# Sending the block outputs of a mixture-of-experts layer to their tokens' places instead of gathering them, with the blocks, the norming, the zeros and the first scores moved

## The chip, the cores and the metric

The kernel runs on one core of one Trainium2 chip. The core has a matrix engine (TensorE, PE in the profile, with PEld for its weight loads), three further engines (VectorE or DVE, ScalarE or ACT, GpSimd or POOL), a queue engine (SyncE or SP) that here only issues transfers, and 16 DMA engines that all queues share. PE, DVE, ACT, POOL and SP each run their own instructions strictly in order and wait for one another on semaphores. The metric is the time of one execution in microseconds (us), as the median of several runs.

## The reference

The input `x` has 8 batches of 512 tokens of 128 features. Four layers follow one another, each of the form

```python
xn = layernorm(x)                 # per token, no gain or bias
x = x + attention_L(xn) + ffn_L(xn)
```

Layer 0: causal attention with 16 heads of 8 features, and a mixture of 16 experts of which each token uses 4:

```python
logits = -sum((x[:, :, None] - keys) ** 2, -1) + x @ rw.T + rb
topv, topi = top_k(logits, 4);  w = softmax(topv)
hidden = gelu(x @ w1[e].T + b1[e]);  out[e] = hidden @ w2[e].T + b2[e]   # 128 -> 512 -> 128
fused = sum over the 4 chosen e of w[e] * out[e]
```

Layer 1: linear attention (8 heads of 64, a decayed running sum over the tokens, a gate), and a mixture of 8 experts of which each token uses one, weighted by its probability:

```python
a, g = split(x @ w1[e], 2);  y = (silu(a) * g) @ w2[e]                  # 128 -> 2*512 -> 128
```

Layer 2: causal attention and an adapter that each batch chooses out of 8; layer 3: attention with a position bias and two of 8 small networks per batch. Layers 2 and 3 are not touched by the change. All arithmetic is in float32.

## The kernel before

**Attention of layer 0.** A *unit* is one batch and one group of four heads: 8 x 4 = 32 units, numbered 4b + g. `stream` (L747) works through them in six steps each. In its steps a unit gets transposed scores (L628), their exponentials on ACT (L669), the products with the values (L687), and at the unit's end a copy (L698) and a division (L721, L724). The row maxima that the exponentials need come from a first set of scores (L556, with the causal mask by L574) and DVE's maxima (L588); this first set runs AHEAD = 5 units in front. The loads of heads for both sets (`sq`, `sk`, `tq`, `tk`) are issued on SP by `load` (L541). In units whose `select` is true, the diagonal is masked on POOL by an affine select (L673) rather than on PE.

**Dispatch to the experts** is the class `Dispatch` (L199 and on), used once for layer 0 (`d0`) and once for layer 1 (`d1`):

- `route` (L260) finds the chosen experts of a batch on DVE, `count` (L308) numbers the tokens of each expert, and `plan` (L329) gives each expert a whole number of *blocks* of 256 tokens (79 blocks for layer 0, 23 for layer 1).
- `fill` (L230) writes zeros over the last block of every expert and over the unused tail in the DRAM table `tok`, by DMAs on SP whose addresses are read into registers (L225, L253).
- `place` (L369) computes each token's slot, and `scatter` (L393) sends the normed rows to their slots: one POOL indirect DMA for 128 rows (L396), 128 of them for layer 0 and 32 for layer 1.
- `owners` (L349) computes which expert each block belongs to. It compares running block counts with the block numbers `kk`, which POOL writes by an iota (L355). `weights` (L287) computes the mixing weights.
- `tokens` (L403) loads a block from `tok` on SP (L406), and waits for the scatters. `expert` (L411) loads the block's weights (L415).
- A block is turned (`turn_tokens`, L434), multiplied (L965 and L967 hold the hidden layer of layer 0, L1284 that of layer 1), and `out_product` (L443) makes the output on PE (L448), adds the bias on DVE (L452, layer 0) or copies on ACT (L454, layer 1) into one of two `ys` buffers, and stores the rows as they stand to the DRAM table `y` by SP (L455).
- `gather` (L418) brings back the rows of 128 tokens by POOL indirect DMAs, one for each choice (L422, 160 in all), and `combine` (L427) adds them to `x` with their weights on DVE (L430, 128 rows of 128 features each, 4 per batch and tile in layer 0).

**Order of the work.** For PE, DVE and ACT the order of instructions is written out by hand (`tc.manual_schedule`, L1547); SP's and POOL's order is chosen by the scheduler of the framework, from the program and its buffers. Tiles with the same tag share a fixed number of buffers, so that a tile waits until an earlier one with its tag has been read. `start0` (L870) norms, routes, plans, fills, places and scatters for layer 0 at the very start; normed rows come from DVE for batches 0 and 1 and from POOL for the others (`apply`, L175). Then `stream` runs the 32 units. `at0(u, h, f)` attaches other work to step h of unit u: the next batch's projections (for batch b at unit 4(b-2)), `owners` at unit 1, `weights` at unit 2. The blocks of layer 0 run inside the units 13 to 22 (`START, SPAN = 13, 10`, so `END0` is 23), 79 blocks in ten units.

From unit 23 on, *spots* are counted: one per step, first over the rest of layer 0's units (`FIRST1 = (32 - END0) * 6`, 54 spots), then six for each of the 32 units of layer 1 (`unit1`, L1310), and two more units. `at_spot(s, f)` attaches work to a spot: the gathers of layer 0 at spots 3n, their combines at 3n + 1 two gathers later (32 each, to spot 100), layer 1's routing of batch b at spot 12b + 17, its plan at 108, its blocks from 140, every three spots, its gathers and combines after the last block. The normed rows of layer 1 are put into DRAM (`xd`, L1068) and read back twice: by `reload` (L1082) as `xc` for the scatters and as `xr` by `again1` (L1108) for the attention of the next batch. Both use the tag `xs`. A layer-1 unit ends with `add1` (L1252, L1260).

Of the kernel before, what the change touches and what calls it, by code (L numbers as in the profile page):

```python
# [10 lines left out]
F32 = mybir.dt.float32  # L11
# [8 lines left out]
P = 128  # L20
# [10 lines left out]
BT = 256  # L31

# [6 lines left out]
def network(ctx: ExitStack, tc: tile.TileContext, io: dict):  # L39
# [59 lines left out]
    steps256 = const.tile([P, 16], F32, name="steps256")  # L99
    nmx = [const.tile([P, NI, P], F32, tag=f"nmx{k}", name=f"nmx{k}") for k in range(2)]  # L100
# [16 lines left out]
    def tables_routing():  # L117
# [11 lines left out]
            before, before, pattern=[[-1, 16], [1, 16]], compare_op=ALU.is_ge, fill=1.0, base=0, channel_multiplier=0  # L129
        )  # L130
# [43 lines left out]

    def apply(b, engine, xn):  # L175
        mv, rt = normal[b]
        for i in range(NI):
            engine.tensor_scalar(
                xn[:, i, :], x[b][:, i, :], mv[:, i, 0:1], rt[:, i : i + 1], ALU.subtract, ALU.mult
            )  # L180
        return xn
# [5 lines left out]
    def turn_norm(L, b, xn, tag="xnT", bufs=3):  # L187
        pt = one_of(f"xt{L}_{b}")
        for i in range(NI):
            nc.tensor.transpose(pt[:, blk(i)], xn[:, i, :], ident)  # L190
        xnT[b] = wk.tile([D, T], F32, tag=tag, name=f"xnT{L}_{b}", bufs=bufs)
        nc.scalar.copy(xnT[b], pt)
# [3 lines left out]
    NOSYNC = mybir.DependencyInfo(mybir.DependencyClass.NoSync, mybir.DependencyReason.DATA)  # L196

    class Dispatch:


        def __init__(self, L, E, K, nblk, room):
# [14 lines left out]
            self.tok = dram.tile([nblk * BT + 4096 + E * BT, D], F32, name=f"tok{L}", tag=f"tok{L}", bufs=1)  # L216
            self.y = dram.tile([nblk * BT, D], F32, name=f"y{L}", tag=f"y{L}", bufs=1)
            self.scattered, self.fetched, self.got = [], [], {}
# [11 lines left out]
        def fill(self, zero):  # L230


            E = self.E
            wide = zero.shape[1] // D * P
            tails = -(-(self.nblk - NB * NI * P * self.K // BT) * BT // wide)
            last = small.tile([1, 16], F32, tag="f_last", name=f"fl{self.L}", bufs=1)[:, :E]
            nc.vector.tensor_scalar(last, self.end, float(BT), -float(BT), ALU.mult, ALU.add)
            sp = small.tile([1, 16], F32, tag="f_sp", name=f"fsp{self.L}", bufs=1)[:, :E]
            nc.vector.tensor_scalar(sp, steps256[0:1, :E], float(self.nblk * BT + 4096), None, ALU.add)
            nc.vector.tensor_tensor(sp, sp, last, ALU.subtract)  # L240
            at = small.tile([1, E + 8], F32, tag="f_at", name=f"fat{self.L}", bufs=1)
            nc.vector.scalar_tensor_tensor(at[:, :E], self.nb[0:1], 0.0, sp, ALU.is_equal, ALU.mult)
            nc.vector.tensor_tensor(at[:, :E], at[:, :E], last, ALU.add)
            for r in range(tails):
                nc.vector.tensor_scalar(
                    at[:, E + r : E + r + 1], self.end[:, E - 1 : E], float(BT), float(wide * r), ALU.mult, ALU.add
                )
            ai = small.tile([1, E + 8], mybir.dt.int32, tag="f_ai", name=f"fai{self.L}", bufs=1)
            nc.vector.tensor_copy(ai[:, : E + tails], at[:, : E + tails])
            for e in range(E + tails):  # L250
                n = BT if e < E else wide
                r = self.register(ai[0:1, e : e + 1], self.nblk * BT + 4096 + E * BT - n)
                d = nc.sync.dma_start(  # L253
                    self.tok[bass.ds(r, n)].rearrange("(p a) d -> p (a d)", p=P), zero[:, : n // P * D]
                ).ins
                self.fetched.append(d.name)
                tc.declare_no_dep(d, group=f"fill{self.L}", reason="zeros over zeros")
                tc.add_to_no_dep_group(f"fill{self.L}", d)

        def route(self, b, lg):  # L260
# [10 lines left out]
            idx = small.tile([P, NI, K], F32, tag="r_idx", name=f"ridx{n}")  # L271
# [57 lines left out]
        def plan(self):  # L329
            L, E = self.L, self.E  # L330
            n = self.run[:, NB]
            gt = small.tile([P, E, 16], F32, tag="r_tab", name=f"gt{L}", bufs=1)
# [8 lines left out]
            bf = small.tile([P, E, E], F32, tag="r_tab", name=f"bf{L}", bufs=1)  # L341
# [3 lines left out]
            self.end = small.tile([1, E], F32, tag="r_end", name=f"end{L}", bufs=1)  # L345
            nc.vector.tensor_tensor(self.end, self.base[0:1], nb[0:1], ALU.add)
            nc.vector.tensor_scalar(self.base, self.base, float(BT), None, ALU.mult)

        def owners(self):  # L349

            L, E = self.L, self.E
            le = wk.tile([P, 2 * T], F32, tag="p", name=f"le{L}", bufs=6)[0:1].bitcast(BF16)[:, : self.nblk * E]
            le = le.rearrange("p (k e) -> p k e", e=E)
            kk = small.tile([1, self.nblk], F32, tag="r_kk", name=f"kk{L}", bufs=1)
# [5 lines left out]
                self.end.unsqueeze(1).to_broadcast([1, self.nblk, E]),  # L360
                kk.unsqueeze(2).to_broadcast([1, self.nblk, E]),
                ALU.is_le,
            )
            ef = small.tile([1, self.nblk], F32, tag="r_ef", name=f"ef{L}", bufs=1)
            nc.vector.tensor_reduce(ef, le, AX.X, ALU.add)
            self.eb = small.tile([1, self.nblk], mybir.dt.int32, tag=f"r_eb{L}", name=f"eb{L}", bufs=1)
            nc.vector.tensor_scalar(self.eb, ef, float(E - 1), None, ALU.min)

        def place(self, b0, n):  # L369
# [3 lines left out]
            at = small.tile([P, 4 * NI * 16], F32, tag="r_at", name=f"at{name}", bufs=1)[:, : n * NI * E]  # L373
# [1315 lines left out]
```

## Time and profile before

| What | Value |
|---|---|
| runs | 2900.8, 2902.2, 2893.13 us; median 2900.8 |
| profiled execution | 2873.46 us |
| its span, first to last instruction | 2871.7 us, mean granted TensorE clock 0.876 |
| PE busy | 2446.5 us, 85% of the span |
| DVE / ACT / POOL busy | 1429.6 / 1191.7 / 616.1 us |
| POOL: scatters of layer 0 to their slots; gathers | L396 x128, 123.6 us; L422 x160, 153.5 us |
| DMA | 292.71 MB, mean 102 GB/s |

The profile comes from one execution, which was 27 us shorter than the median of the runs. Busy time is the time in which an engine works on an instruction; a row such as "x128 | 123.6, 965" gives the number of instructions, their busy time in us and the mean of one in ns. In a list of waits, "A L1 <- B L2: 10.0, 3, 5.0" means that instructions of line L1 on engine A waited for line L2 on engine B for 10.0 us in total, 3 times, at most 5.0 us. SPq is SP's queue of DMA issues. Lines are those of the kernel before, unless said otherwise.

### The profile page before, as it was taken

What the parts mean: (1) busy time and instruction counts of PE and PEld (TensorE: products, weight loads), DVE (VectorE), ACT (ScalarE), POOL (GpSimd) and SP (SyncE); (2) the same over time, 40 slices, a digit from 0 to 9 for tenths busy, and PEclk for the clock granted to TensorE, in tenths of its full rate; (3) what the DMA queues carried; (4) which work ended last, traced back from release to release, by engine and by line L of the source; (5) the groups of instructions that cost most, each with busy time, mean ns of one, the idle gap of its engine ahead of it and who ended that gap; (6) DMA issues with size and microseconds to landing.
All of it is one profiled execution on the core that took longest, in us unless ns stands there. A gap on an engine that the chain in (4) does not pass through costs nothing.

```text
span 2871.7 us, 45766 instructions
## 1 busy us (share of the span) xinstructions
PE 2446.5 (85%) x17798; PEld 1601.0 (56%) x17798; DVE 1429.6 (50%) x2976; ACT 1191.7 (41%) x1740; POOL 616.1 (21%) x897
## 2 busy tenths in 40 slices
PE   5660889989998868589998888888889999999999
PEld 3330447878775546477776544444445555555554
DVE  5630443333335456345555866655556655555550
ACT  1020335546555422223332145545444545555556
POOL 7475000000004553400003432222222000000000
PEclk6565789999998888799998979999888989999999
DMA  4342225666663211413322332322222222123211
GB/s 130 126 140 84 89 89 177 204 185 192 189 183 107 80 47 41 131 44 97 92 74 67 107 95 95 101 91 91 91 91 82 94 83 83 59 83 98 83 49 35
DMA packets 219000, 292.71 MB, mean 102 GB/s; under 512 B 27170, under 2 KB 112674, under 8 KB 218658
## 3 DMA queue, kind: packets, MB, share of 16 engines
q1 hardware_dynamic: 208546, 268.81, 30.2%
q0 software_dynamic: 10240, 20.99, 2.4%
q8 instruction: 141, 2.31, 0.3%
q14 instruction: 73, 0.60, 0.1%
HBM read 204.90 MB, written 84.80 MB: 101 GB/s over the span
## 4 chain that ended last, share of the span: by engine, by line
PE 69%; ACT 10%; POOL 7%; issue 6%; DVE 5%; DMA 2%; SPq 1%; ACTq 0%; DVEq 0%; POOLq 0%
PE o L687 11%; PE y L448 7%; ACT p L669 6%; PE t L628 5%; PE s L556 5%; PE h L965 5%; POOL tok L396 5%; PE t L640 5%; PE t L659 4%; PE h L1284 3%; PE s L574 2%; PE s L583 2%; PE qk L1126 2%; PE o L1213 2%; PE ot L707 2%
## 5 line engine op out<-in xcount | busy, mean ns | idle before, releaser
L588 DVE TENSOR_REDUCE max<-s 128x2 f32<-128x1024 f32 (+3 forms) x768 | 716.3, 953 | 676.8 <-PE s L574 447.9
L669 ACT ACTIVATE p<-t 128x1024 f32<-128x1024 f32 (+1 forms) x384 | 338.1, 881 | 572.3 <-PE t L640 286.0
L556 PE MATMUL s<-sk,sq 32*128 32x512 f32 (+3 forms) x1536 | 336.6, 463 | 115.0 <-DMA sk<-apartk 89.5
L628 PE MATMUL t<-tq,tk 32*128 32x512 f32 (+3 forms) x1536 | 339.9, 472 | 81.0 <-ACT p L669 74.0
L669 ACT ACTIVATE p<-t,rsc 128x1024 f32<-128x1024 f32 x256 | 281.1, 1116 | 216.6 <-PE t L659 162.1
L687 PE MATMUL o<-p,vpad 128*32 128x512 f32 (+3 forms) x3072 | 335.5, 580 | 0.2 <-ACT p L669 0.2
L556 PEld LDWEIGHTS s<-sk,sq 32*128 32x128 f32 x1536 | 146.4, 201 | 290.5 <-issue 183.8
L673 POOL TENSOR_SCALAR_AFFINE_SELECT p<-p 128x256 f32<-128x256 f32 x336 | 132.5, 407 | 740.1 <-ACT p L669 739.9
L640 PE MATMUL t<-mT,pick 32*128 32x512 f32 (+3 forms) x1536 | 262.0, 368 | 0.0
L422 POOL DMA_INDIRECT g<-y,slot x160 | 153.5, 959 | 471.0 <-issue 342.6
L628 PEld LDWEIGHTS t<-tq,tk 32*128 32x128 f32 x1536 | 143.9, 198 | 171.6 <-ACT p L669 132.7
L687 PEld LDWEIGHTS o<-p,vpad 128*32 128x32 f32 x3072 | 97.5, 127 | 157.2 <-issue 137.6
L448 PE MATMUL y<-ring_w,ring_h 128*128 128x128 f32 x1264 | 156.8, 281 | 15.4 <-DVE lowk L501 8.3
L448 PEld LDWEIGHTS y<-ring_w,ring_h 128*128 128x128 f32 x1264 | 148.6, 195 | 23.6 <-DVE lowk L501 8.7
L640 PEld LDWEIGHTS t<-mT,pick 32*128 32x128 f32 x1536 | 157.2, 205 | 2.4 <-issue 1.9
L965 PE MATMUL h<-t,ring_w 128*128 128x256 f32 x632 | 148.2, 383 | 2.6 <-issue 2.6
L396 POOL DMA_INDIRECT tok<-xn,slot x128 | 123.6, 965 | 70.3 <-issue 38.4
L574 PE MATMUL s<-mask_qk,ident_bf 128*128 128x128 bf16 (+1 forms) x768 | 137.1, 266 | 0.0
L659 PEld LDWEIGHTS t<-anti,hk 128*128 128x128 f32 x768 | 100.2, 199 | 50.6 <-issue 50.6
L965 PEld LDWEIGHTS h<-t,ring_w 128*128 128x128 f32 x632 | 116.5, 192 | 17.3 <-issue 3.4
L967 ACT ACTIVATE ring_h<-h,ring_w 128x256 f32<-128x256 f32 x316 | 119.4, 499 | 4.2 <-ACT ring_h L967 2.1
L659 PE MATMUL t<-anti,hk 128*128 128x128 f32 x768 | 118.9, 293 | 0.0
(276 smaller groups left out, 3470.5 us busy)
## 6 DMA issues: line engine op xcount, KB each, us to landing
ring_w<-in_f_w SPq DMA_DIRECT2D x79, 322.0 KB, 3.6
sq<-apartq SPq DMA_DIRECT2D x96, 256.0 KB, 2.6
tq<-apartq SPq DMA_DIRECT2D x96, 256.0 KB, 2.9
sk<-apartk SPq DMA_DIRECT2D x96, 256.0 KB, 4.1
tk<-apartk SPq DMA_DIRECT2D x96, 256.0 KB, 4.0
ring_w<-in_f_w SPq DMA_DIRECT2D x79, 256.0 KB, 3.6
xb<-tok SPq DMA_DIRECT2D x102, 128.0 KB, 4.4
y<-y SPq DMA_DIRECT2D x102, 128.0 KB, 2.1
```

Source lines behind the costliest of these rows:

```text
L396: d = nc.gpsimd.indirect_dma_start(self.tok, bass.IndirectOffsetOnAxis(self.slot[:, b, i, k : k + 1], 0), xs[:, i, :], None).ins
L422: nc.gpsimd.indirect_dma_start(g[:, k, :], None, self.y, bass.IndirectOffsetOnAxis(self.slot[:, b, i, k : k + 1], 0))
L448: nc.tensor.matmul(py[:, blk(t)], lhsT=h(f, t), rhs=w2[:, blk(f)], start=(f == 0), stop=(f == 3))
L556: nc.tensor.matmul(s[:, j, off : off + width], lhsT=q[r : r + 32, blk(i)], rhs=k[r : r + 32, :width], start=(n == 0), stop=not more, skip_ ...
L574: nc.tensor.matmul(s[:, j, c0:c1], lhsT=ident_bf, rhs=mask_qk[:, : c1 - c0], start=False, stop=True, skip_group_check=True,)
L588: nc.vector.tensor_reduce(m[:, i, g, 2 * pr : 2 * pr + 2], s[:, :, off : off + width], AX.X, ALU.max, negate=True)
L628: nc.tensor.matmul(s[:, h, off : off + T - q0], lhsT=k[r : r + 32, blk(j)], rhs=q[r : r + 32, q0:T], start=(n == 0), stop=False, skip_grou ...
L640: nc.tensor.matmul(s[:, h, off : off + T - q0], lhsT=pick[r : r + 32, g, :], rhs=mT[r : r + 32, q0:T], start=False, stop=not more, skip_gr ...
L659: nc.tensor.matmul(s[:, k, blk(i)], lhsT=self.bias[1 + part][:, h, blk(kind - i - 2)], rhs=self.bias[0], start=False, stop=(i == kind - 2 ...
L669: nc.scalar.activation(p, s[:, :, :width], AF.Exp, scale=self.scale)
L687: nc.tensor.matmul(st[b, g][blk(h, 32), q0:T], lhsT=vpad[b % 2][:, j, g * HG + h, :], rhs=st[b, g, kind, h // 2][:, h % 2, off : off + T - ...
L965: nc.tensor.matmul(s[:, f], lhsT=w1[:, blk(f)], rhs=xt, start=True, stop=True, skip_group_check=True)
```

## The change

- **Places travel with the rows.** A row of `tok` has 136 floats in place of 128. Layer 0's normed rows carry the four places that their four results will have, and the four expert numbers; layer 1's carry their token's place. When a block has been turned, `places` (three small DVE instructions in layer 0, one in layer 1) picks the place that belongs to the block's expert.
- **Sends and fetches in place of stores and gathers.** `out_product` no longer stores; `send` writes the 256 rows of a block to their tokens' places in `y` by two POOL indirect DMAs. `fetch` then reads the rows of 128 tokens (layer 0) or of a batch (layer 1) by one plain load on SP, where `gather` stood.
- **The timing table.** Blocks of layer 0 run in units 17 to 26, so 30 spots are left in layer 0; fetches stand at spots 2 + n, combines at 4 + n; layer 1's routing at 4b + 8, its plan at 42, its blocks from 74, every four spots. The units of layer 2's first scores begin at the last 30 spots. `owners` moves from unit 1 to unit 2, `weights` from 2 to 3.
- **Normed rows by ACT** in layers 0 and 1: `apply_act`.
- **First scores between the routing steps.** `start0` takes steps of `stream` (`next(stream0)`) between routing steps, three more of them around plan, fill and place; loads of tokens and fetches get an order-only dependence on the last head load issued (`latest`).
- **Zeros by index**: `fill` computes row numbers on DVE and writes the zeros by eight POOL indirect DMAs (four in layer 1) of 128 rows of 4352 bytes.
- `plan`, `place` and `owners` use the shared tag `p` for their temporaries; `owners` works on 128 partitions.

```diff
+ROW = D + 8
+    def apply_act(b, xn):
+        mv, rt = normal[b]
+        nm = small.tile([P, NI], F32, tag="nm", name=f"nm_{b}")
+        nc.vector.tensor_scalar(nm, mv[:, :, 0], -1.0, None, ALU.mult)
+        for i in range(NI):
+            nc.scalar.activation(xn[:, i, 0:D], x[b][:, i, :], AF.Identity, bias=nm[:, i : i + 1])
+        for i in range(NI):
+            nc.scalar.activation(xn[:, i, 0:D], xn[:, i, 0:D], AF.Copy, scale=rt[:, i : i + 1])
...
     def fill(self, zero):
-                d = nc.sync.dma_start(
-                    self.tok[bass.ds(r, n)].rearrange("(p a) d -> p (a d)", p=P), zero[:, : n // P * D]
+            for j in range(n + self.tails):
+                d = nc.gpsimd.indirect_dma_start(
+                    self.tok.rearrange("(r a) d -> r (a d)", a=8),
+                    bass.IndirectOffsetOnAxis(fx[:, j : j + 1], 0), zero, None,
                 ).ins
...
     def owners(self):
-            le = wk.tile([P, 2 * T], F32, tag="p", name=f"le{L}", bufs=6)[0:1].bitcast(BF16)[:, : self.nblk * E]
+            le = wk.tile([P, 2 * T], F32, tag="p", name=f"le{L}", bufs=6).bitcast(BF16)[:, : self.nblk * E]
-            kk = small.tile([1, self.nblk], F32, tag="r_kk", name=f"kk{L}", bufs=1)
+            kk = wk.tile([P, 2 * T], F32, tag="p", name=f"kk{L}", bufs=6)[:, : self.nblk]
             nc.gpsimd.iota(
                 kk, pattern=[[1, self.nblk]], base=0, channel_multiplier=0, allow_small_or_imprecise_dtypes=True
             )
...
     def tokens(self, k):
-            xb = wk.tile([P, 2 * D + 1], F32, tag="xb", name=f"xb{self.L}_{k}", bufs=4)[:, : 2 * D]
+            xb = wk.tile([P, 2 * ROW], F32, tag="xb", name=f"xb{self.L}_{k}", bufs=4)
+            if latest and not self.fetched:
+                tc.add_manual_dep(d, latest[-1], NOSYNC, reason="behind the loads of heads")
+        def places(self, k, xb):
+            n = BT // P
+            at = xb[:, :, D]
+            if self.K > 1:
+                m = small.tile([P, n, self.K], F32, tag="h_m", name=f"hm{self.L}_{k}")
+                nc.vector.scalar_tensor_tensor(
+                    m, xb[:, :, D + 4 : D + 4 + self.K], self.ef[:, k : k + 1], xb[:, :, D : D + self.K],
+                    ALU.is_equal, ALU.mult,
+                )
+                at = small.tile([P, n], F32, tag="h_r", name=f"hr{self.L}_{k}")
+                nc.vector.tensor_reduce(at, m, AX.X, ALU.add)
+            home = small.tile([P, n], mybir.dt.uint32, tag="h_u", name=f"hu{self.L}_{k}", bufs=8)
+            nc.vector.scalar_tensor_tensor(home, loose, float(k * BT), at, ALU.add, ALU.max)
+            self.home[k] = home
+        def send(self, k, ys):
+            home = self.home.pop(k)
+            for t in range(BT // P):
+                d = nc.gpsimd.indirect_dma_start(
+                    self.y, bass.IndirectOffsetOnAxis(home[:, t : t + 1], 0), ys[:, t, :], None
+                ).ins
+        def fetch(self, b, i=None):
+            d = nc.sync.dma_start(g, src).ins
+            for s in self.back[-16:]:
+                tc.add_manual_dep(d, s.name, SYNC, reason="rows are sent first")
-        def gather(self, b, i):
-            for k in range(self.K):
-                nc.gpsimd.indirect_dma_start(
-                    g[:, k, :], None, self.y, bass.IndirectOffsetOnAxis(self.slot[:, b, i, k : k + 1], 0)
-                )
...
-        nc.sync.dma_start(dst.rearrange("(t p) d -> p t d", p=P), ys)
+        return ys
...
-    START, SPAN = 13, 10
+    START, SPAN = 17, 10
...
     def start0():
         for b in range(NB):
+            if b >= 1:
+                for _ in range(2):
+                    next(stream0)
-            chosen[b] = d0.route(b, logits(0, b, kw, lb0, 16))
+            chosen[b] = d0.route(b, logits(0, b, kw, lb0, 16), xn0[:, b, :, D + 4 : D + 8])
-            if b:
+            if b >= 1:
+                for _ in range(2):
+                    next(stream0)
                 d0.count(b - 1, chosen[b - 1])
         d0.count(NB - 1, chosen[NB - 1])
+        next(stream0)
         d0.plan()
         d0.fill(zero)
+        next(stream0)
         d0.place(0, 4)
...
-    at0(1, 2, d0.owners)
-    at0(2, 2, d0.weights)
+    at0(2, 2, d0.owners)
+    at0(3, 2, d0.weights)
...
-    for n in range(len(fetch) + 2):
-        if n < len(fetch):
-            at_spot(3 * n, d0.gather, *fetch[n])
-        if n >= 2:
-            at_spot(3 * n + 1, d0.combine, *fetch[n - 2])
+    for n, (b, i) in enumerate(fetch):
+        at_spot(2 + n, d0.fetch, b, i)
+        at_spot(4 + n, d0.combine, b, i)
     for b in range(NB):
-        s = 12 * b + 17
+        s = 4 * b + 8
-    s = 12 * (NB - 1) + 24
+    s = 4 * (NB - 1) + 14
...
+    EACH = 4
     for k in range(d1.nblk + 1):
-        at_spot(s + 3 * k, hidden1, k, 0)
+        at_spot(s + EACH * k, hidden1, k, 0)
```

## The prediction

> **What bounds the kernel now.** I read the page's slices first, then windows of 40 us, then the waits of the stretches in which PE is idle, then single lines' start times.
>
> ```profile
> PE   5660889989998868589998888888889999999999
> POOL 7475000000004553400003432222222000000000
> PEclk6565789999998888799998979999888989999999
> ```
>
> One slice is 71.8 us. PE is the bound almost everywhere; it is not in slices 1 to 4 (0 to 287 us) and in the dips of slices 13 to 17. From slice 24 (layers 2 and 3, from about 1661 us) PE stands at 9, and the change does not reach there.
>
> ```profile
> 160.00:200.00 40.00, 35.33 (x252) 19.14 (x248) 22.22 (x42) 15.05 (x20) 30.40 (x31) 0.70 0.39 137
> 200.00:240.00 40.00, 0.83 (x8) 0.52 (x8) 0.85 (x2) 0.77 (x2) 30.52 (x32) 0.54 0.16 52
> 240.00:280.00 40.00, 0.15 (x4) 0.18 (x4) 0.00 (x0) 0.00 (x0) 21.33 (x24) 0.50 0.32 107
> 280.00:320.00 40.00, 34.67 (x258) 19.41 (x260) 17.46 (x25) 14.78 (x19) 0.00 (x0) 0.80 0.38 117
> ```
>
> The columns are the window, its length, and busy us of PE, PEld, DVE, ACT, POOL, then granted clock, DMA share, GB/s. From 202 to 280 us three engines stand still and POOL alone works. Why, the waits of 130 to 300 us and SP's own say:
>
> ```profile
> DVE max L588 <- PE s L574: 118.2, 23, 79.9
> ...
> PE s L556 <- DMA sk<-apartk: 78.8, 1, 78.8
> ```
>
> ```profile
> SPq L406 <- DMA tok<-xn,slot: 96.1, 3, 93.7
> ```
>
> SP's first token load (L406) waits 93.7 us for the last of POOL's 128 scatters, and the head loads (`sk`) of unit 8 are queued behind it. The scatters' own rows, first in 60 to 200 us, then in 200 to 280 us:
>
> ```profile
> L396 POOL DMA_INDIRECT tok<-xn,slot x74 | 71.9, 971 | 53.9 <-DMA tok<-room 31.6 <-issue 21.9 <-DMA tok<-xn,slot 0.3
> ```
>
> ```profile
> L396 POOL DMA_INDIRECT tok<-xn,slot x54 | 51.7, 957 | 16.5 <-issue 16.5
> ```
>
> One takes 0.96 us and 0.30 us of issue: 128 start 1.264 us apart, from 105.6 to 267.9 us. They wait 31.6 us for the zeros (`tok<-room`, 78 to 102 us).
>
> The other weak stretch is the end of layer 0 and the start of layer 1 (windows of 840 to 880, of 1000 to 1080 and of 1160 to 1240 us):
>
> ```profile
> 840.00:880.00 40.00, 38.25 (x326) 29.52 (x325) 14.30 (x32) 22.18 (x41) 4.90 (x11) 1.00 0.46 140
> ...
> 1000.00:1040.00 40.00, 23.61 (x172) 14.95 (x172) 19.56 (x72) 13.81 (x21) 16.52 (x18) 0.82 0.12 35
> 1040.00:1080.00 40.00, 28.08 (x214) 20.46 (x212) 24.72 (x78) 10.37 (x16) 23.43 (x25) 0.84 0.20 56
> ...
> 1160.00:1200.00 40.00, 23.92 (x176) 18.63 (x175) 14.67 (x32) 7.95 (x12) 23.52 (x25) 0.78 0.50 163
> 1200.00:1240.00 40.00, 27.18 (x167) 19.73 (x167) 9.74 (x17) 8.54 (x13) 7.51 (x8) 0.66 0.19 55
> ```
>
> The first is a block stage, PE-bound at clock 1.00. The last two hold layer 1's scatter stall (waits of 1130 to 1245 us): the reload `xr` of `again1(3)` finds no free buffer while `xc` tiles wait to be scattered.
>
> ```profile
> PE xt L190 <- DMA xr<-xd: 21.0, 1, 21.0
> ```
>
> **The change part by part.** The sum is made against the profiled execution, 2873.5 us (span 2871.7). The three runs have a median of 2900.8, 27.3 us more; I add that at the end. A difference under about 0.3% (9 us) can't be told from none.
>
> **Routing and scores interleaved.** Before, routing runs at one batch in 5.2 us (POOL's normed rows set it; DVE's own part is about 4.6), the plan stands at 75 us, and the first 30 score steps follow from 84.4 to 124.4 us, 1.33 us each. After, ACT norms (DVE keeps one small `nm` a batch, ACT eight instructions, at most eight times the 0.69 us of an L499 activation; ACT is busy 2.9 of 40 us there, so hidden), and 29 score steps stand ahead of `fill`'s index in DVE's order. Their lower price is DVE's: 16 maxima took 12.05 us, a unit's six steps 6.2, so 30 us; the upper is 29 x 1.33 = 39. Plan: 75 + 30 to 39, less 0 to 5 for the lost POOL bound, = 100 to 114 us; I take 105. The same scores vanish from behind the plan, so no work is lost; what is lost is that the scatters start later.
>
> **Zeros by index.** Eight POOL DMAs with 4.46 MB in place of SP's 20 with about the same. Before they took 24 us. At the page's best slice, 204 GB/s, 21.9 us; at the 163 GB/s of the window 80 to 120, 27.4. Equal within 3 us. POOL waits for them, SP's register loads go. Scatters start at 105 + 3 + 25 = 133 us (bounds 122 to 150).
>
> **Scatters and the new wait.** 128 x 1.264 = 162 us: done issuing at 295 (284 to 312). Now the step that decides. `owners` builds its block numbers `kk` by an iota on POOL (L401 after). Before, `kk` had a small buffer and its iota ran at 26 us. After, it lives in a shared `p` buffer, and in the order of POOL's instructions it stands behind all 128 scatters; `le` (L404 after) on DVE waits for it at the third step of unit 2. DVE runs in order: maxima, normings and the lows of `project` are queued behind `le`; PE waits for the maxima, ACT for PE. So SP's wait goes (the token loads now stand behind the head loads of unit 21), and DVE's takes its place, until 295 + 1 for the iota + 3 for `le` and its sum = 299 us. Before, everything resumed at 280 us with unit 3 in hand (L698 at 291); after, at 299 with unit 2 half done, 1.3 units behind, and a plain unit takes 17.5 us (311, 328, 346, 362). Cost: 19 + 1.3 x 17.5 = **+42 us** (30 to 60 by the bounds above). The stall itself grows from 78 to some 145 us (the interleaving brings unit 2 to 153 us instead of about 184), which is where the gain of the start goes.
>
> **Blocks four units later, sends.** A block unit takes 40 to 43 us, PE-bound, units 16 and 20 53 to 54 (the next batch is projected there and waits for `apartq`). Of the new ten only unit 20 projects a batch; the wait of unit 16 falls among plain units, where it shows no such cost: **-12** (-12 to 0). Per block one SP store goes (landing 2.1 us) and POOL gets two sends of 1.26 us in a unit's slack; `places` adds three tiny DVE instructions, about 0.5 us x 79, beside PE-bound work: 0; if that cover were gone, 40. `ys` has two buffers; a send may stand behind an affine select that waits for ACT (L673, 0.41 us), and the bias add of the block after next waits for the send's landing (2.25 us from POOL's start): **+10** (0 to 40).
>
> The row of 136 floats: its price per scatter or send is not in the trace; 0.96 us is for 128 rows of 512 B, both for scatters and for gathers. Lower end 0; upper end if POOL's time went with the bytes: 6%, +10 us on 128 scatters. I take 0, as issue seems to go by the row. The Trainium skill ("DMA: Bandwidth & Descriptors", section "How a descriptor splits into AXI transactions") says that a run starting off a 256 B boundary costs extra transactions; by it a 544 B row that starts off one moves up to 24 beats instead of 16, an estimate from that page. It would lengthen a token load by half, which is issued four blocks ahead, and leave the sum as it is. The same page (section "SWDGE vs HWDGE vs iDMA") says that DVE can lock POOL out while it writes descriptors. Here the scatters took 971 ns beside a busy DVE and 957 beside an idle one; by the rule sends beside DVE's work would cost more, by the rows nothing.
>
> **Fetches in place of gathers.** 160 POOL gathers (0.96 us each) go; 40 plain loads on SP come. The combines (4 x 0.351 us each) stay, but 32 of them now come at one spot each, 28 in units 27 to 31, with six routings of about 4 us among them: DVE gets about 28 x 1.4 + 6 x 4 = 63 us beside its own work in units that took 64 us before. **+15** (0 to 30). In exchange layer 1's first units carry none of it: they took 13 to 17 us (1068, 1085, 1098, 1118, 1132 at L1260), bare ones 13.5 to 15: **-14** (-20 to 0).
>
> **Layer 1.** Its plan is 66 spots earlier, but `again1(1)` wants its `xr` buffer 11 spots behind it, where before it had 17; the scatters of 32 x 1.26 = 40 us hold it as before: 26 us of stall becomes about 38: **+12** (0 to 20). 23 blocks at 1.5 a unit cost what 2 a unit did, about 4.5 us a block. The gather tail (1540 to 1660 us, PE 31.5 to 33.3 of 40) goes: **-10** (-20 to 0).
>
> Sum: 42 - 12 + 10 + 15 - 14 + 12 - 10 = +43; 2873.5 + 43 = 2916.5 in a profiled run; + 27.3 = **2944** against the median.
>
> **Rivals.** *Faster: the weak stretch closes.* The nine windows from 880 to 1240 us hold 88.7 us of idle PE, and PE at 37 of 40 would leave 27: 62 us to be won; the tail another 15. If the earlier routing and plain fetches win all of it, 42 - 12 - 62 - 15 = -47: 2854. For it: POOL's gathers wait on buffers there (19.5 us in 1000 to 1040). Against it: the same DVE work is packed tighter, and the layer-1 scatters remain. It decides once the terms behind the start add up to less than -42.
>
> *The DVE wait binds, and rows cost more.* If the wider rows or POOL's double work in the blocks bind at the upper ends (+10 scatters, +40 `ys`, `places` uncovered +40), 43 + 10 + 30 + 40 = +123: 3024. Against it: POOL is busy 2 to 4 tenths in the block slices.
>
> *No change.* The start's +42 is met by a half of the weak stretch: 2901.
>
> *The change does what it is said to at the start, and DVE is not held*: the SP wait of 78 us goes, the start's gain of 31 us stays: about -109 + 1 = 2793. Only if the iota ran ahead of the scatters, which the instruction order excludes; I give it 2 in 100.
>
> **How the numbers follow.** Forecast 0.58, slower rival 0.10, faster rival 0.24, unheld start 0.02, no change 0.06. The range leaves out half of the slower rival, the unheld start and a part of the faster rival's low end: 2846 to 3000. The forecast's own range is 2915 to 2980. Faster 0.26, same 0.06, slower 0.68.
>
> **What would show it.** In the profile after: `le` on DVE waiting for POOL's `kk` about 140 us; no wait of SP's token load; POOL's scatters from 133 to 295 us at 1.26 us; PE near 0 in 160 to 295; unit 3 finished near 334; PE over 39 of 40 in blocks, from about 560 us; no L422-like gathers. I am wrong if the scatters end well before 280 or cost another price, or if the stretch behind the blocks gets 60 us shorter.

## The result and the profile after

The changed kernel takes 3006.9 us (median; 2999.97 to 3013.12) against 2899.7 us: 1.039 times the time before, 95% interval 1.035 to 1.044. It is slower, as forecast, but by 107 us where the forecast had 43, and it lies 7 us above the range. The profiled execution has a span of 3006.3 us, granted clock 0.853.

The slices of the page after, 75.2 us each:

```profile
PE   6702888889898864788888888888889999999999
POOL 4475000343433204011110132222222100000000
PEclk6655778999999756899999979899888989889999
```

The third slice (150 to 225 us) has PE at 0. The windows over the start (columns as in the prediction: window, length, busy us of PE, PEld, DVE, ACT, POOL, granted clock, DMA share, GB/s):

```profile
120.00:160.00 40.00, 26.55 (x202) 13.90 (x199) 11.17 (x15) 11.51 (x14) 30.24 (x33) 0.70 0.42 133
160.00:200.00 40.00, 0.00 (x0) 0.00 (x0) 0.00 (x0) 0.00 (x0) 30.51 (x32) 0.50 0.16 56
200.00:240.00 40.00, 0.00 (x0) 0.00 (x0) 0.00 (x0) 0.00 (x0) 30.28 (x32) 0.50 0.16 56
240.00:280.00 40.00, 0.00 (x0) 0.00 (x0) 2.71 (x2) 0.00 (x0) 28.37 (x31) 0.50 0.15 52
280.00:320.00 40.00, 35.56 (x254) 20.25 (x254) 20.47 (x42) 14.66 (x20) 0.00 (x0) 0.71 0.44 142
```

and what DVE waited for there (waits of 100 to 400 us):

```profile
DVE le L404 <- POOL kk L401: 128.4, 1, 128.4
PEld t L714 <- DVE max L674: 127.5, 1, 127.5
```

There is one wait of 128.4 us, of `le` for `kk`, and PE waits behind DVE. The scatters' and the fills' own rows (minimum, median and maximum in ns, first and last start):

```profile
L442 POOL DMA_INDIRECT tok<-xn,slot x128: 954/958/967, 115.7 to 276.0; - x128
```

```profile
L299 POOL DMA_INDIRECT tok<-room,ffx x8: 947/954/1378, 100.3 to 110.0; - x8
```

A second place is the block stage (windows of 640 to 720 us, then one of the kernel before, where PE stood at 38 to 39.5 of 40 away from a change of batch):

```profile
640.00:680.00 40.00, 34.88 (x248) 29.89 (x247) 15.48 (x46) 18.06 (x37) 19.90 (x25) 0.91 0.58 183
680.00:720.00 40.00, 37.18 (x283) 29.98 (x282) 14.70 (x38) 21.77 (x44) 14.34 (x19) 1.00 0.50 155
```

```profile
680.00:720.00 40.00, 38.71 (x303) 32.28 (x302) 13.93 (x35) 22.76 (x44) 3.16 (x8) 1.00 0.65 196
```

The third is the end of layer 0 (units 28 to 31, after, then before):

```profile
1040.00:1080.00 40.00, 25.90 (x166) 16.26 (x166) 23.00 (x111) 20.07 (x46) 4.62 (x11) 0.54 0.31 93
1080.00:1120.00 40.00, 23.24 (x150) 14.01 (x146) 24.56 (x121) 15.38 (x35) 3.24 (x4) 0.54 0.26 79
```

```profile
960.00:1000.00 40.00, 37.14 (x306) 21.97 (x304) 16.82 (x78) 17.51 (x23) 27.32 (x29) 0.74 0.32 95
```

Neither PE nor DVE is full after the change, and the granted clock is 0.54, where the same units had 0.74 and 0.82 before (959 to 1023 us; the window of 1000 to 1040 us stands in the prediction). The engines wait for each other in turn, and the granted clock is lower besides.

The account is made from the start of the copy of `oT` (L698 before, L784 after), with which every unit ends. Each row is the time that the stage took in the two profiled executions:

| Stage | before, us | after, us | difference |
|---|---|---|---|
| to unit 11 | 431 | 452 | +21 |
| units 12 to 27 (all blocks in both) | 528 | 561 | +33 |
| units 28 to 31 | 64 | 115 | +51 |
| layer 1, to the first unit of layer 2 | 664 | 679 | +15 |
| the rest | 1185 | 1199 | +14 |
| span | 2872 | 3006 | +135 |

Layers 2 and 3 hold no edit apart from the start of layer 2's first scores, so I put the last +14 down to the executions: the profiled one of before was 27 us shorter than its median. A second profile of each kernel (experiment 5) supports it. Its five differences are +20, +36, +51, +26 and +4 us: the first three stages repeat within 3 us, while layer 1 and the rest trade 10 us, because layer 1 of the kernel before took 664 us in one profile and 653 in the other. What is to be explained is some 120 to 130 us in the first four stages.

### The profile page after: what moved, and what is told of

It reads as the page before. It is cut to its first block, busy times and chain, and to the rows that moved or that the text cites. A ratio compares the mean times of both kernels' runs of the same rounds, so it can differ in the third digit from the quotient of the medians.

```text
span 3006.3 us, 45917 instructions
## 1 busy us (share of the span) xinstructions
PE 2504.7 (83%) x17798; PEld 1628.0 (54%) x17798; DVE 1451.4 (48%) x3211; ACT 1230.2 (41%) x1884; POOL 653.5 (22%) x947
## 4 chain that ended last, share of the span: by engine, by line
PE 46%; ACT 8%; DVE 3%; issue 3%; DMA 1%; POOL 0%; SPq 0%; DVEq 0%; ACTq 0%; POOLq 0%
PE o L773 8%; ACT p L755 4%; PE s L642 4%; PE t L745 4%; PE t L714 3%; PE t L726 3%; PE h L1390 2%; PE qk L1230 2%; PE s L669 2%; PE o L1317 2%; PE s L1252 1%; PE y L533 1%; PE rc L1507 1%; PE v L1219 1%; PE s L660 1%
## 5 line engine op out<-in xcount | busy, mean ns | idle before, releaser
L755 ACT ACTIVATE p<-t,rsc 128x1024 f32<-128x1024 f32 x256 | 280.8, 1115 | 227.7 <-PE t L745 172.8
L773 PE MATMUL o<-p,vpad 128*32 128x512 f32 (+3 forms) x3072 | 348.4, 599 | 0.2 <-ACT p L755 0.2
L480 POOL DMA_INDIRECT y<-y,hu x204 | 196.0, 961 | 512.9 <-ACT y L539 351.5
L533 PE MATMUL y<-ring_w,ring_h 128*128 128x128 f32 x1264 | 155.0, 280 | 10.8 <-DVE y L537 6.2
L1065 PE MATMUL h<-t,ring_w 128*128 128x256 f32 x632 | 162.1, 409 | 0.0
L533 PEld LDWEIGHTS y<-ring_w,ring_h 128*128 128x128 f32 x1264 | 146.9, 194 | 18.3 <-DVE y L537 8.5
L1065 PEld LDWEIGHTS h<-t,ring_w 128*128 128x128 f32 x632 | 126.1, 208 | 18.1
```

Source lines behind the costliest of these rows:

```text
L480: d = nc.gpsimd.indirect_dma_start(self.y, bass.IndirectOffsetOnAxis(home[:, t : t + 1], 0), ys[:, t, :], None).ins
L533: nc.tensor.matmul(py[:, blk(t)], lhsT=h(f, t), rhs=w2[:, blk(f)], start=(f == 0), stop=(f == 3))
L755: nc.scalar.activation(p, s[:, :, :width], AF.Exp, scale=self.scale)
L773: nc.tensor.matmul(st[b, g][blk(h, 32), q0:T], lhsT=vpad[b % 2][:, j, g * HG + h, :], rhs=st[b, g, kind, h // 2][:, h % 2, off : off + T - ...
L1065: nc.tensor.matmul(s[:, f], lhsT=w1[:, blk(f)], rhs=xt, start=True, stop=True, skip_group_check=True)
```

## Experiments

Unless said otherwise, a kernel is the changed one with the edits named, and ratios are to the kernel before on the same chip. Experiments 1 to 3 ran on one chip (the first chip below), 4, 5 and 6 on a second, a third and a fourth; on the second, the kernel before itself took 3014 us.

**1. `kk` in a buffer of its own.**

```diff
-            kk = wk.tile([P, 2 * T], F32, tag="p", name=f"kk{L}", bufs=6)[:, : self.nblk]
+            kk = small.tile([P, self.nblk], F32, tag="r_kk", name=f"kk{L}", bufs=1)
```

> The changed kernel with one edit: kk, the list of block numbers in owners, has a small buffer of its own again, so that POOL can write it ahead of the 128 scatters. Theory (the wait of DVE's le on POOL's iota is a stall of its own, 128.4 us in the trace of the changed kernel, and nothing else stands behind it): the wait is gone, unit 3 finishes near 180 us instead of 313, and the time falls by 110 to 130 us from 3007 to about 2885. Rival (the scatters hold something else as well, such as the token loads or POOL's adds, so that the stall only moves a few units on): unit 10 finishes within 60 us of the 436 of the changed kernel, and the time falls by less than 60 us.

Measured 2892.1 us, ratio 1.001 (0.9985 to 1.003): 115 us less. Unit 3 finishes at 185 us, unit 10 at 312. Its windows, while POOL goes on scattering:

```profile
160.00:200.00 40.00, 33.94 (x266) 18.56 (x268) 18.96 (x37) 16.14 (x22) 30.47 (x32) 0.84 0.67 220
200.00:240.00 40.00, 36.74 (x264) 18.99 (x256) 17.35 (x31) 12.18 (x16) 30.32 (x32) 0.66 0.40 131
```

POOL's column is that of the changed kernel, and PE works at 34 to 37 of 40, as in the windows behind the stall. So the tag of one buffer was the whole stall, and nothing else that holds the units up waited for the scatters. This one line takes the change back to no difference.

**2. More buffers for block outputs, and stores in place of sends.**

```diff
-        ys = wk.tile([P, n, D], F32, tag="ys", name=name, bufs=2)
+        if int(name.split("_")[1]) % 2:
+            ys = wk.tile([P, NI * NH * (HD + 1)], F32, tag="gat", name=name, bufs=3)
+            ys = ys[:, : n * D].rearrange("p (t d) -> p t d", t=n)
+        else:
+            ys = wk.tile([P, n, D], F32, tag="ys", name=name, bufs=2)
```

> The changed kernel with more buffers for block outputs: odd blocks take one of the three gat buffers instead of one of the two ys buffers, so that a block output waits for the send of four or more blocks before. In the changed kernel a block unit takes 46 to 48 us against 40 to 41 in the kernel before, and DVE waits for the sends' landing. Theory (two buffers with POOL's sends, which stand behind affine selects, are what costs 6 us a block unit): block units fall to 40 to 42 us, the total by 40 to 60 us. Rival (the sends' transfers, or the lost granted clock, or the places on DVE cost it): block units stay at 46 to 48 us, total within 10 us of 3007.

```diff
         def send(self, k, ys):
-            home = self.home.pop(k)
-            for t in range(BT // P):
-                d = nc.gpsimd.indirect_dma_start(
...
+            nc.sync.dma_start(self.y[k * BT : (k + 1) * BT].rearrange("(t p) d -> p t d", p=P), ys)
...
-            d0.places(k, xb)
-            d1.places(k, xb)
```

> The changed kernel with block outputs stored as they stand by SP, as in the kernel before, and without places; the fetches read rows of y that are not the token's, so the results of both expert layers are left wrong, and POOL's sends and the three DVE instructions a block are left out. Theory (sends are what lengthens block units): block units 40 to 42 us, total 40 to 60 us below 3007; layer-1 units with blocks get 1 us shorter too. Rival (the block units are longer for another reason, such as rows of 544 B, ACT's norming or the transfers of that stage): block units stay at 46 to 48 us.

Measured 2972.3 us (1.028, 1.022 to 1.033) with more buffers and 2976.6 (1.031, 1.026 to 1.035) with stores: 35 and 30 us less than the changed kernel, under the 40 to 60 forecast for both. Units 17 to 25 take 40 to 43 us in both (54 and 53 in unit 20), against 46 to 48 (53). So sends cost nothing in themselves once they have buffers, nor do `places`. Layer 1 takes 678 us with sends and with stores, so the 1 us a unit that was forecast for it was not there. What DVE's bias add waited for from 520 to 1000 us (us, times), first in the changed kernel, then with more buffers:

```profile
  PE y L533: 95.7, 54
  DMA y<-y,hu: 42.5, 16
  DMA tq<-apartq: 24.6, 6
```

```profile
  PE y L533: 117.9, 73
  DMA y<-y,hu: 5.4, 4
```

Waiting for landed sends falls from 42.5 to 5.4 us, and the 24.6 us put down to `tq` loads go too. The add reads no `tq`, so that row was probably another wait under the name of what came last.

**3. Layer 1's routing and layer 0's combines at half the density.**

```diff
-        at_spot(2 + n, d0.fetch, b, i)
-        at_spot(4 + n, d0.combine, b, i)
+        at_spot(2 * n, d0.fetch, b, i)
+        at_spot(2 * n + 4, d0.combine, b, i)
...
-        s = 4 * b + 8
+        s = 8 * b + 12
...
-    EACH = 4
+    EACH = 3
...
-        at_spot(s + EACH * k + 3, turn1t, k + 1)
+        at_spot(s + EACH * k + 2, turn1t, k + 1)
```

> The changed kernel with layer 0's fetches and combines every two spots instead of every spot, layer 1's routing every eight spots instead of four (first at 12), its plan at spot 74 instead of 42, its blocks every three spots instead of four. Theory (units 28 to 31 take 115 us instead of 64 because routing and combines are packed so tightly that each step of their chain from engine to engine has only one spot): units 28 to 31 take 70 to 90 us, the total falls by 25 to 50 us. Rival (the tables of layer 1 and its setup, which moved with END0 into the last four units of layer 0, make these units long): they stay at 105 to 115 us, the total within 15 us of 3007.

Measured 2994.7 us, 1.036 (1.031 to 1.041): 12 us less than the changed kernel, under the forecast. Units 28 to 31 take 76 us, as the theory had it, but layer 1 takes 697 instead of 679: with three spots a block, its units with two blocks take 25 to 30 us, where before they took 22 to 25. The setup and tables of layer 1 are in the same units here as in the change, so they are not the cause of the long units 28 to 31. Routing and combines were thinned out together; what each of them costs alone is not shown here.

**4. Four kernels on the second chip.** The whole table of the kernel before (`START, SPAN = 13, 10`, and the spots of the lines that the diff removes, with `fetch` for `gather` and its combine at 3n + 7):

> The changed kernel with the whole timing table of the kernel before: blocks of layer 0 from unit 13 (START 13, 54 spots left in layer 0), fetches where the gathers stood (3n) and combines at 3n + 7, layer 1's routing at 12b + 17, its plan at 108, its blocks from 140 every three spots in the old order, layer 2 begun 7 spots behind them; sends, plain fetches, ACT norming, zeros by index, interleaved scores and the wait for kk stay. Theory (the tighter table costs 50 us in units 28 to 31 and 10 to 20 in layer 1, and saves 12 at a change of batch in the blocks): the total falls by 40 to 65 us to 2940 to 2967, units 28 to 31 take 64 to 70 us. Rival (the fetches and the ACT norming lengthen that stretch, not the table): units 28 to 31 stay over 100 us and the total within 20 us of 3007.

Layer 1's normed rows by DVE:

```diff
-        hold[b] = apply_act(b, wk.tile([P, NI, D], F32, tag="aT", name=f"xn1_{b}", bufs=3))
+        hold[b] = apply(b, nc.vector, wk.tile([P, NI, D], F32, tag="aT", name=f"xn1_{b}", bufs=3))
```

> The changed kernel with layer 1's normed rows for routing made by DVE as before (four instructions of 0.35 us a batch) in place of nm and eight ACT instructions. Theory (in units 28 to 31 the routing chain waits for ACT, which does eight instructions a batch there beside its exponentials): units 28 to 31 take 95 to 105 us instead of 115 and the total falls by 10 to 20 us. Rival (DVE, on which combines and routing meet, is what holds these units): they stay or grow by up to 6 us, the total within 10 us of 3007.

The pieces of a layer-1 block in the old order:

```diff
-        at_spot(s + EACH * k + 1, hidden1, k, 1)
-        at_spot(s + EACH * k + 2, out1, k - 1)
-        at_spot(s + EACH * k + 3, turn1t, k + 1)
+        at_spot(s + EACH * k + 1, out1, k - 1)
+        at_spot(s + EACH * k + 1, turn1t, k + 1)
+        at_spot(s + EACH * k + 2, hidden1, k, 1)
```

> The changed kernel with the pieces of a layer-1 block in the old order inside its four spots: first half of the hidden layer, then the output of the block before and the next turn, then the second half (the change has both halves side by side, then output, then turn). Theory (side by side, the second half waits on ACT and DVE, which is why 1.5 blocks a unit take 22 us, as long as two blocks did before): units with blocks take 20 to 21 us, the total falls by 15 to 30 us. Rival (they are long for another reason, such as the sends or the granted clock, which is 0.91 to 0.99 there): units stay at 22 us, the total within 8 us of 3007.

All of table, `kk` and buffers:

> The changed kernel with kk in a small buffer of its own, odd block outputs in gat buffers, and the whole timing table of the kernel before. If the three causes add up (115 us for kk and 35 for the buffers as measured one by one, 50 for the table as forecast), 3007 - 200 = about 2807 us, 3% faster than before. If they overlap, for example because an early end of the start only moves blocks into a stretch in which something else is late, the total stays over 2840.

Measured 3009, 3043, 3049 and 3010 us beside 3014 for the kernel before (ratios 0.998, 1.011, 1.012, 1.000, each about 0.005 either way). The times in the four expectations could not be tested: all four kernels, that with a free `kk` too, finish unit 0 at 245 to 255 us instead of 133. PE's instructions there, in the last kernel, and in the kernel of experiment 1 on the first chip (start, busy time, instruction, in brackets the idle time before it):

```profile
156.97 0.37 PE L740 MATMUL t<-mask_kq,ident_bf 128*128 128x256 bf16 x1 [2.43 <-issue]
159.77 0.47 PE L646 MATMUL s<-sk,sq 32*128 32x384 f32 x1 [2.43 <-issue]
```

```profile
148.41 0.60 PE L714 MATMUL t<-tq,tk 32*128 32x128 f32 x4
148.73 0.23 PE L642 MATMUL s<-sk,sq 32*128 32x128 f32 x2
```

On that chip, while POOL scatters (116 to 277 us), PE first gets a matmul every 2 to 2.8 us, from about 134 to 168 us in the last kernel, and then none until 247 us. DVE and ACT stand still as well (waits of the last kernel from 95 to 320 us; "issue" and "remote" mean that the profile shows no instruction and no transfer that ended the wait):

```profile
ACT p L759 <- remote: 164.1, 3, 116.8
DVE max L678 <- remote: 153.2, 3, 110.2
PE t L718 <- issue: 88.7, 6, 78.5
```

A second halt follows from 251 to 291 us; from 300 us on PE is normal again. So the expectations of experiment 5, which speak only of matmuls that come slowly, leave out most of the lost time. Within the chip, later stages can still be compared: units 28 to 31 take 63 us with the old table, 113 with the new one, 97 with the new one and norming by DVE; layer 1's units with blocks take 21.4 us in the old order and 22.7 in the new.

**5. The change again, the kernel before with a profile, and two sums of edits, on a third chip.**

> The changed kernel as it is, beside the kernel before on the same chip, since the last four runs went to a chip on which the kernel before itself took 3014 us instead of 2893 and on which PE's matmuls came one in 2 to 2.8 us while POOL's scatters ran. If this chip is like the first, the ratio is 1.035 to 1.044 and the wait for kk 128 us. If it is like the second, both kernels lie over 2990 us and the ratio is near 1.01, since both lose the time of the scatters.

> The kernel before, for its profile on this chip. On a chip like the first: PE idle from 202 to 280 us only, its span 2870 to 2895 us. On a chip like the second the theory (while POOL writes indirect transfers, PE's instructions reach it slowly there, whichever kernel runs) expects unit 0 to finish after 230 us, with PE's waits named issue, and the gathers from 880 to 1160 us to lengthen the units there; the rival (only the changed kernels meet it) expects unit 0 at 161 us.

> The same kernel as j_best (kk in a buffer of its own, odd block outputs in gat buffers, the whole timing table of the kernel before). On a chip like the first: if the three causes add up, 2795 to 2825 us, 0.965 to 0.978 of the kernel before; block units 40 to 42 us, units 28 to 31 64 to 70 us, unit 10 near 312 us. On a chip like the second: 1.00 again.

> The changed kernel with two of the edits: kk in a buffer of its own and odd block outputs in gat buffers; the table of the change stays. On a chip like the first the two add up to 150 us: 2850 to 2865 us, 0.985 to 0.99 of the kernel before, and j_again should be 40 to 60 us faster than this by the table alone. On a chip like the second: within 1% of the changed kernel there.

Measured: the change 3009.0 us (1.042, 1.036 to 1.048), with a wait for `kk` of 125 us; the kernel before 2883.9, in its profile unit 0 at 159 us. So this chip is like the first, and whether the kernel before meets the same halts on the second chip was left untested. `kk` and buffers take 2843.2 us (0.984, 0.978 to 0.990), with the old table as well 2814.3 us (0.975, 0.968 to 0.981). The edits add up: 166 us for the first two (150 forecast, from the 115 and 35 measured singly). The table gives 29 us more, not 40 to 60: units 28 to 31 fall from 113 to 63 us, but the units from 12 to 27 take 535 us instead of 516, since unit 16, a second change of batch among blocks, takes 54 us again, and layer 1 stays at 678 us.

**6. Norming and order again, on a fourth chip like the first.**

> The same kernel as n_dve1: layer 1's normed rows for routing made by DVE. On the second chip units 28 to 31 took 96 us against 112 in l_order there. Theory (the chain of routing waits for ACT): units 28 to 31 take 95 to 102 us against 115, and the ratio to the kernel before is 1.031 to 1.037 against 1.039 to 1.042 for the change. Rival: 115 us and the ratio of the change.

> The same kernel as l_order: the pieces of a layer-1 block in the old order within its four spots. On the second chip its block units took 21.4 us against 22.7 in n_dve1. Theory (the order costs 1.3 us a unit, 16 units): the ratio is 1.031 to 1.036. Rival (the sends of POOL cost it): units of 22 us and the ratio of the change, 1.039 to 1.042.

> j_again's kernel with layer 1's normed rows by DVE. With the table of the kernel before a routing has 12 spots, so if ACT's norming costs only where the chain is tight, this is within 6 us of j_again's ratio, 0.968 to 0.981; if it costs anywhere, it is 10 us or more faster, 0.964 to 0.971.

Norming by DVE: 2997.7 us, 1.038 (1.030 to 1.046). Units 28 to 31 take 96 us and layer 1 673; the interval of the ratio holds both expectations, the stages agree with the theory. Old order of the pieces: 2994.3 us, 1.036 (1.029 to 1.043), layer 1 668 us instead of 679. The waits of 1253 to 1530 us in the change, and in this kernel:

```profile
DVE h L1398 <- ACT h L1394: 89.2, 30, 5.3
ACT h L1394 <- PE y L533: 82.9, 17, 5.8
```

```profile
DVE h L1398 <- ACT h L1394: 36.8, 26, 3.1
```

With the halves side by side, ACT's second half stands behind PE's output of the block before; in the old order that row (`ACT h L1394 <- PE y L533`) is gone. The ratios of these two kernels overlap the change's own; their verdict rests on the stages.

All four edits together (`kk`, buffers, old table, DVE norming in layer 1): **2785.1 us, 0.965 (0.958 to 0.972)**, 3.5% faster than the kernel before and 7% than the change. Layer 1 takes 652 us. With the same table and norming by ACT it took 678 on the third chip and 664 and 668 on the second, so norming by ACT seems to cost there even where routing has twelve spots; but these are other chips, and the kernel before itself took 664 and 653 us there in its two profiles. The ratios' intervals overlap.

The whole gain lies in the start: unit 11 ends at 327 us, against 431 and 435 in the two profiles of the kernel before, and everything behind it takes 2454 us against 2441 in both. So sends, fetches and the rest of the change show no gain after unit 11 even here. How the gain of the start divides between the interleaved scores, the zeros by index and the loads that no longer wait was not measured.

The slices of this kernel:

```profile
PE   6788899998988676899988888988899999999999
POOL 5477044343410005011111422222222000000000
```

The hole at slices 1 to 4 is gone in spite of POOL's scatters; the dips that are left are slice 14, the passage to layer 1, and slice 16, layer 1's scatters (two neighbouring unit ends of layer 1 lie 37 us apart, at 1077 and 1115 us).

## Why the prediction was right and wrong

**In short.** That the change is slower, and the wait that makes it so at the start, were forecast rightly. The sum failed in three terms, which were too small: the two `ys` buffers (+10, measured +46), units 28 to 31 (+15, measured +51) and layer 1 (-12, measured +15 or, in the second pair of profiles, +26). The start was priced 21 us too high, which hid a part of that; that the total came as near to the range as it did is luck.

**The bound before, and the wait that moves: right.** `le` on DVE waits for `kk` behind the scatters; 128 us, forecast some 145. Scatters of rows of 544 B took 0.958 us each, as the sends of rows of 512 B in the block stage did (L480, 0.958): the row's price is nothing, as taken. Two rules of the Trainium skill were weighed there. By "DMA: Bandwidth & Descriptors", section "How a descriptor splits into AXI transactions", rows that start off a 256 B boundary cost extra beats; here token loads of 136 KB landed in 2.7 us, against 4.4 for 128 KB before. That is no clean test, since they stand beside other transfers and the kernel before had 3.7 in its second profile, but no price shows. By its section "SWDGE vs HWDGE vs iDMA", DVE in one of its modes locks POOL out of the memory that POOL writes descriptors to; sends took 0.958 us where DVE was busy 15 of 40 us, and whether DVE was then in that mode, no trace says.

**Its size: too high.** Scatters began at 115.7 us, not 133: the zeros took 15 us, not 25 (they moved 4.46 MB at nearly 290 GB/s, above the best slice I had bounded them by), and they began 8 us sooner than the 108 us I had for them. DVE went on at 277 us. Cost +21, not +42.

**Blocks: mis-sized, above its upper bound.** The term "+10 (0 to 40)" for `ys` was 46: 459 us from unit 15 to unit 25 in the change, 413 with more buffers (the median of the whole kernel fell by 35). PE, forecast at over 39 of 40, stood at 34.9 and 37.2. I had named the wait (a send behind an affine select, then its landing, with two buffers) and put it near its lower end without a reason. An `ys` buffer is wanted again two blocks, about 10 us, later, and POOL, in whose order the sends stand, waits for ACT in front of an affine select by up to 11 us (waits of the change, 600 to 740 us):

```profile
POOL p L759 <- ACT p L755: 30.7, 3, 11.4
```

With more buffers POOL still waits there (36.2 us, at most 10.1), but DVE waits little for it (the 5.4 us of experiment 2). Against 424 us for the ten units before that correspond (12 to 21), the 413 agree with the -12 for the change of batch.

**Units 28 to 31: the mis-sized term.** "+15 (0 to 30)" measured +51. I counted DVE's busy time, 63 us, and asked whether it fits. DVE was busy 47.6 of 80 us in 1040 to 1120. What filled the time is the chain of one routing, which goes from engine to engine (DVE, POOL, ACT, PE, DVE) with one spot for each step:

```profile
ACT xn L206 <- DVE nm L204: 32.7, 7, 8.6
PEld xt L226 <- ACT xn L208: 16.1, 11, 4.2
```

These are waits of the change from 1004 to 1130 us. Dividing the density by two took 39 us off (experiment 3), the old table 49 (experiments 4 and 5), norming by DVE 18 (experiment 6). I had called ACT's norming hidden, costed it at the start only, and not looked at where it stands in this chain.

**Layer 1: sign missed.** -14 + 12 - 10 was forecast, +15 measured (+26 in the second pair of profiles). The scatter stall grew as forecast (51 us between two unit ends instead of 40; PE waits 33.3 us for `xr` instead of 21.0). I had not costed the new order of a block's pieces, since the number of blocks was the same, and had taken a block at 4.5 us whatever the units: 1.5 blocks a unit took the 22 us that two had taken. Order gives 11 us of it, and it is not the sends: with stores layer 1 takes 678 us too, and with the old order and table (experiments 4 and 5) a unit with two blocks takes 22.5 us as before, with sends. Norming by DVE gives 6 with the tight table, and perhaps 12 to 25 with the loose one. The -10 for the tail without gathers did not show where it can be seen: from the last unit with blocks to layer 1's last addition, the old table takes 143 to 147 us with fetches in four profiles, and 139 and 147 us with gathers in the two of the kernel before.

**The rivals.** The slower one named the buffers as one of three bounds and priced them nearly right (+40, measured +46), together with two that were nothing; that its 3024 us lie near the result is luck. The faster one fell: the weak stretch as a whole got longer. The unheld start, put at 2793 us, was measured in experiment 1: unit 11 ended 102 us sooner than in the kernel before (109 were forecast), and the total still came to no change, since the other stages had lost what it won.

## What to carry to other kernels

A temporary that moves from a small buffer of its own to a shared tag can push a harmless instruction behind everything that an in-order engine has queued: look for the place of each producer in the order of its engine, not only for its cost. A buffer count that is enough for a transfer of 2 us from a free queue may not be for the same transfer from a queue that waits for something else first; count from the time the tile is written to the landing, queueing included. And a stretch without a full engine isn't free room: work packed into it pays the length of its chain, so count the steps of the chain and the places that the order of work gives them, not only the busy time.

## What the runs showed of the hardware

One POOL indirect DMA of 128 rows took 0.95 to 0.96 us of POOL whatever the row: 0.954 for the zeros' 4352 B, 0.958 for 544 B, 0.958 for 512 B. The eight with 4352 B moved 4.46 MB in 15 us.

On one of four chips, all four kernels lost their start while POOL's 128 indirect transfers ran: PE got a matmul every 2 to 2.8 us and then none for 78.5 us, while DVE stood still for 109 to 119 us and ACT for 116 to 126, and the trace names nothing in the program that held them. The transfers themselves took their usual 0.958 us. The block units with sends took 48 to 51 us there away from a change of batch, even with the extra buffers that made them 40 to 43 us elsewhere, and 47 to 50 with two buffers. The kernel before took 4% longer on that chip. The trace doesn't say what holds the engines; that it is POOL's transfers is argued from the two stretches that slow down, not shown.
